# Two query tiles share one output projection in a local-attention loop, and the feed-forward's stages are placed anew

## The chip, the cores and the metric

The program runs on one core of a Trainium2 chip. A core has five engines that run side by side, each with its own queue worked off in order: TensorE (PE, matrix products, with its weight loads shown apart as PEld), VectorE (DVE), ScalarE (ACT), GpSimd (POOL) and SyncE (SP), which here issues DMA transfers. Matrix products land in PSUM, a memory of eight banks; one bank holds 512 fp32 values in each of 128 partitions. The metric is the device time of one execution in microseconds (us); lower is better.

## The reference, cut to what matters

The network adds eight residual blocks to x of shape (4, 512, 128). The change touches one of them, a six-layer local transformer (`_L2_ffn_ref`):

```python
for i in range(DEPTH):                       # 6
    x = attn_layer(shift_tokens(x), Wqkv[i], q_scale[i], k_scale[i], Wo[i]) + x
    x = ffn_layer(shift_tokens(x), ln_g[i], ln_b[i], W1[i], b1[i], W2[i], b2[i]) + x
```

```python
def attn_layer(x, Wqkv, qs, ksc, Wo):
    qkv = x @ Wqkv                           # 128 -> 3 * 1024
    ...
    q = l2norm(q) * qs                       # and k; 16 heads of 64
    ...
    out = local_attention(q, k, v)           # windows of 32, each sees itself and the one before
    out = out.transpose(0, 2, 1, 3).reshape(b, n, INNER)
    return out @ Wo                          # 1024 -> 128

def ffn_layer(x, g, bln, W1, b1, W2, b2):
    ...                                      # layer norm
    hg = xn @ W1 + b1                        # 128 -> 2 * 341
    a, gate = jnp.split(hg, 2, -1)
    return a * jax.nn.gelu(gate, approximate=False) @ W2 + b2
```

The last product of the attention, `out @ Wo`, is the one whose form changes.

## The kernel before, in words

The program has a first and a middle part, the local transformer, and a last part. The first, middle and last parts are ordered by a planner (class `Plan`), from costs written into the code; they are not changed. The local transformer (`local_transformer`) is ordered by hand: its instructions go to each engine's queue in the order in which the loop at L2040 emits them.

The data of one batch row lie in `Y[b]`, features on partitions and the 512 tokens along the row; the upper 64 features stand one column to the right, which is the shift of the tokens. A row has four tiles of 128 tokens (`T.tt` = 0 to 3); with four rows and six layers there are 96 tiles. The loop over n is a pipeline. Trip n works on three tiles: T = tile n makes its queries, keys and values (`queries_or_keys` L1779, `rotate` L1791, `normalise` L1812, `values` L1849); T1 = tile n-1 turns them to features (`turned` L1830), makes its scores and the first steps of its softmax (`scores` L1876, `softmax` L1899); T2 = tile n-2 averages, divides, is turned to features and projected (`probabilities`, `average`, `normalised`, `attended`, `project_out` L1945, `residual` L1951). With two trips to drain there are 98.

A fourth worker is the feed-forward of a finished row, F. It is spread over four trips, its phases: `divmod(n - 6, 4)` gives row and phase. Each phase has two places in the trip, a first one after the queries and a second one at its end (`ff_stage` L2018):

- phase 0: first, the row is transposed and its moments are found (`ff_moments`); after the residual, the norm is applied on DVE (`ff_norm`, L523);
- phase 1: first, the norm's result is turned (`ff_turn`); second, the gates of chunks 0 and 1 with their Gelu on ACT (`ff_gate`, L1983);
- phase 2: first, the gate of chunk 2; second, the up products of chunks 0 and 1 and their multiplication on DVE (`ff_up`, L1994 and L1997);
- phase 3: first, up of chunk 2; second, the down product and its addition to Y (`ff_down`, L2006, and `add_y`, L1723).

Chunks have 128, 128 and 85 of the 341 inner features. ACT loads another table before the first Gelu of a row and goes back after the last. The last row of the last layer has its feed-forward in the last part (`last_feed_forward`).

PSUM is held in four tags. `mm` and `tr` have two single banks each: queries and keys, and transposes and values. `sc` and `av` (`pair`, with bufs=1) have one buffer of two banks each. In `sc` lie the scores, until DVE has taken the maximum (L1903) and the subtraction (L1904) from them; every feed-forward product takes `sc` too. In `av` lie the averages and then the projection.

On PE a trip runs: queries, P transposes, queries, first feed-forward step, averages, q transposes, keys, averages, k transposes, keys, attn transposes, scores, projection, values, second feed-forward step. On DVE the rotations and divisions come first, then the maximum and the subtraction, then the residual. On ACT, after the softmax's exp (L1909) come the copies of v, a Gelu of the second step, and the next trip's squares (L1788) and P copies (L1914); a rotation on DVE waits for its square.

The projection takes 8 products of 128x128 weights with 128 columns of `aT`; in fp32 PE runs two passes for each, so the profile counts 16.

Of the kernel before, what the change touches and what calls it, by code (L numbers as in the profile page):

```python
# [20 lines left out]
F32 = mybir.dt.float32  # L21
# [13 lines left out]
DEPTH, LH, LD, WIN = 6, 16, 64, 32  # L35
# [204 lines left out]
def tile_kernel(ctx: ExitStack, tc: tile.TileContext, A: dict, out: bass.AP):  # L240
    nc = tc.nc
    V, G, SC, PE, DMA = nc.vector, nc.gpsimd, nc.scalar, nc.tensor, nc.sync
# [43 lines left out]
    def p_tr(*shape):  # L286
        return psum(shape, "tr", 2)
# [54 lines left out]
    for b in range(B):  # L342
        t = xpool.tile([128, NT, D], F32, name=f"x{b}", tag=f"x{b}")
# [26 lines left out]
    with banks(), tc.tile_pool(name="prep", bufs=1) as prep:  # L370
# [26 lines left out]
        t = p_tr(128, B, SK)  # L397
# [3 lines left out]
        t = p_tr(128, 4, D)  # L401
# [3 lines left out]
        t = p_tr(128, 8)  # L405
# [3 lines left out]
        t = p_tr(128, 2, E)  # L409
# [59 lines left out]
    def col(r):  # L469
        return cols[:, r : r + 1]  # L470
# [7 lines left out]
    for i, cap in enumerate((CAP0, CAP3, CAP3)):  # L478
        n = -(-E * cap // 128)
# [101 lines left out]
    def to_features(src):  # L581

        t = p_tr(128, NT, 128)
        for i in range(NT):
            PE.transpose(t[:, i], src[:, i], ident)  # L585
        return t
# [1114 lines left out]
    def local_transformer(Y, lf):  # L1701

        with ExitStack() as es:
# [4 lines left out]
            tp = es.enter_context(tc.tile_pool(name="lt", bufs=2))  # L1708
# [3 lines left out]
            def pair(tag):  # L1712

                t = homes["pair"].tile([128, 2, 512], F32, tag=tag, bufs=1, name=f"ps_{tag}")
                return t

            def add_y(b, t, bias=None):
                for r, o in ((slice(0, 64), 0), (slice(64, 128), 1)):
                    dst = Y[b][r, o : o + S]
                    if bias is None:  # L1720
                        V.tensor_tensor(dst, t[r], dst, ALU.add)
                    else:
                        V.scalar_tensor_tensor(dst, t[r], bias[r], dst, ALU.add, ALU.add)  # L1723
# [213 lines left out]
                )  # L1937

            def attended(T):
                flat = T.attn.rearrange("p k x d -> p k (x d)")  # L1940
                T.aT = tp.tile([128, LH // 2, 128], F32, name="aT", bufs=1)
                for g in range(2):
                    SC.copy(T.aT[:, 4 * g : 4 * g + 4], to_features(flat[:, 4 * g : 4 * g + 4]))

            def project_out(T):  # L1945
                t = pair("av")[:, 0, :128]
                for c in range(8):
                    PE.matmul(t, T.wo[:, c], T.aT[:, c], start=(c == 0), stop=(c == 7))  # L1948
                T.out = t

            def residual(T):  # L1951
                t = T.out
                for r, o in ((slice(0, 64), 0), (slice(64, 128), 1)):
                    dst = Y[T.b][r, 128 * T.tt + o : 128 * T.tt + o + 128]
                    V.tensor_tensor(dst, t[r], dst, ALU.add)


            def ff_moments(F):
                F.t = pair("sc")[:, 0].rearrange("p (a b) -> p a b", b=128)
                for tt in range(NT):  # L1960
                    PE.transpose(F.t[:, tt], Y[F.b][:, 128 * tt : 128 * tt + 128], ident)
                F.xn = lnp.tile([128, NT, D], F32, name="xn")
                SC.copy(F.xn, F.t)
                F.found = moments(F.xn)

            def ff_norm(F):
                layernorm(F.xn, F.xn, F.found)
# [11 lines left out]
            def ff_gate(F, *chunks):  # L1979
                t = pair("sc")  # L1980
                for j, c in enumerate(chunks):
                    n, o = CH_W[c], DI + 128 * c
                    PE.matmul(t[:n, j], F.w1[:, o : o + n], F.xnT, start=True, stop=True)  # L1983
                for j, c in enumerate(chunks):
                    n = CH_W[c]
                    SC.activation(
                        F.h[:n, c], t[:n, j], AF.Gelu, bias=col(R_B1 + (3 + c) * DEPTH + F.i)[:n]
                    )

            def ff_up(F, *chunks):  # L1990
                t = pair("sc")
                for j, c in enumerate(chunks):
                    n, o = CH_W[c], 128 * c
                    PE.matmul(t[:n, j], F.w1[:, o : o + n], F.xnT, start=True, stop=True)  # L1994
                for j, c in enumerate(chunks):
                    n = CH_W[c]
                    V.scalar_tensor_tensor(  # L1997
                        F.h[:n, c], t[:n, j], col(R_B1 + c * DEPTH + F.i)[:n], F.h[:n, c],
                        ALU.add, ALU.mult,
                    )  # L2000

            def ff_down(F):
                t = pair("sc")[:, 0]
                for c in range(3):
                    n = CH_W[c]
                    PE.matmul(t, F.w2[:n, c], F.h[:n, c], start=(c == 0), stop=(c == 2))  # L2006
                add_y(F.b, t, col(R_B2 + F.i))
# [10 lines left out]
            def ff_stage(F, phase, second):  # L2018
                F.w1, F.w2 = loaded[F.i][3:5]
                if phase == 0 and not second:  # L2020
                    ff_moments(F)
                elif phase == 1:
                    ff_gate(F, 0, 1) if second else ff_turn(F)
                elif phase == 2 and second:
                    ff_up(F, 0, 1)
                elif phase == 2:
                    ff_gate(F, 2)
                    SC.preload_act_table_set(EXP_LN)
                elif phase == 3:
                    ff_down(F) if second else ff_up(F, 2)  # L2030

            tiles = [Tile(i, b, tt) for i in range(DEPTH) for b in range(B) for tt in range(NT)]
# [2 lines left out]
            tabs = {0: tables(loaded[0][5])}  # L2037
            swap(0)
            SC.preload_act_table_set(EXP_LN)
            for n in range(len(tiles) + 2):  # L2040
                T = tiles[n] if n < len(tiles) else None
                T1 = tiles[n - 1] if 0 <= n - 1 < len(tiles) else None
                T2 = tiles[n - 2] if 0 <= n - 2 < len(tiles) else None
                m, phase = divmod(n - 6, 4)
                F = rows[m] if 0 <= m < len(rows) else None
                if T:
                    if n % 16 == 7 and T.i + 1 < DEPTH:
                        loaded[T.i + 1] = load(T.i + 1)
                    if n == 4:
                        fill, send, send_back = clear(lnp, 1)  # L2050
                        fill(G)
                        send(DMA)
                        send_back(DMA)
                    if n % 16 == 15 and T.i + 1 < DEPTH:
                        tabs[T.i + 1] = tables(loaded[T.i + 1][5])
                    T.before = tiles[n - 1] if T.tt else None
                    T.w, T.wv, T.wo = loaded[T.i][:3]
                    T.tabs = tabs[T.i]
                    queries_or_keys(T, 0, 0)
                if T2:  # L2060
                    probabilities(T2)
                if T:
                    queries_or_keys(T, 0, 1)
                    rotate(T, 0, 0)
                if F:
                    ff_stage(F, phase, False)
                if T2:
                    average(T2, 0)
                if T1:
                    turned(T1, 0)  # L2070
                if T:
                    queries_or_keys(T, 1, 0)
                if T2:
                    normalised(T2, 0)
                if T:
                    rotate(T, 0, 1)
                if T2:
                    average(T2, 1)
                if T1:
                    turned(T1, 1)  # L2080
                if T:
                    queries_or_keys(T, 1, 1)
                if T2:
                    normalised(T2, 1)
                if T:
                    rotate(T, 1, 0)
                if T2:
                    attended(T2)
                if T and T.tt == NT - 1 and n + 1 < len(tiles):
                    swap(tiles[n + 1].b)  # L2090
                if T1:
                    scores(T1)
                if T:
                    rotate(T, 1, 1)
                if T:
                    normalise(T)
                if T1:
                    softmax(T1)
                if T2:
                    project_out(T2)  # L2100
                    residual(T2)
                if F and phase == 0:
                    ff_norm(F)
                if T:
                    values(T, 0)
                    values(T, 1)
                if F:
                    ff_stage(F, phase, True)
# [95 lines left out]
    with ExitStack() as stay:  # L2204
        yp = stay.enter_context(tc.tile_pool(name="y", bufs=1))
        Y = []
# [32 lines left out]
```

## Time and profile before

| | us |
|---|---|
| median of three runs | 2434.31 (2431.93 to 2436.33) |
| the profiled execution | 2475.2 |
| its span, first to last instruction | 2473.4 |
| PE busy | 2242.8 (91%) |
| DVE busy | 1745.4 (71%) |
| ACT busy | 1291.9 (52%) |
| POOL busy | 1383.7 (56%) |
| L1948, projection, PE | 198.0 in 1536 passes |
| L1786, queries and keys, PE | 398.0 in 768 passes |

In a row of the profile come the line of the code, the engine, what is written and read with its shape, the count, the busy time and the mean of one in ns, and after the second bar the idle time of the engine before these instructions with what ended it. Matmuls overlap one another, so the distance between the starts of two says more than the duration of one. In a timeline the first two numbers are the start and the time until the merged instructions ended, in us; a bracket at the end is the engine's idle time before them and what released it.

### The profile page before, as it was taken

How to read it: one execution, taken by the hardware profiler on the slowest of the kernel's cores; microseconds unless marked ns; L12 is line 12 of the kernel's file. 1: busy time of each engine (PE TensorE's matmuls, PEld its weight loads, DVE VectorE, ACT ScalarE, POOL GpSimd, SP SyncE). 2: the span in 40 equal slices, each digit the busy share in tenths (PEclk: the TensorE clock that was granted, in tenths of full speed). 3: DMA queues.
4: the chain of work that ended last, by engine and by line, in shares of the span. 5: the costliest groups of instructions: out<-in, count | busy, mean ns of one | idle time of the engine just before them, and what ended most of it. 6: DMA issues, size and time to landing. Idle time of an engine off the chain costs nothing.

```text
span 2473.4 us, 86733 instructions
## 1 busy us (share of the span) xinstructions
PE 2242.8 (91%) x37341; PEld 1478.8 (60%) x37341; DVE 1745.4 (71%) x3818; ACT 1291.9 (52%) x2379; POOL 1383.7 (56%) x1948
## 2 busy tenths in 40 slices
PE   7959879968999999999999999999999999988686
PEld 3527644536666666666666666666666666644364
DVE  5626355757788888877887888888888888765522
ACT  3523225535666556666666666566666666533232
POOL 2242232446667666676667667766667666532433
PEclk9969989989999999999999999999999999989688
DMA  7210110015411121111211121111211111120022
GB/s 161 87 42 21 36 42 2 1 51 102 118 29 35 31 60 50 26 35 35 70 35 31 33 79 32 30 35 29 76 35 32 30 35 34 30 78 10 23 75 82
DMA packets 134297, 116.14 MB, mean 47 GB/s; under 512 B 29505, under 2 KB 102700, under 8 KB 133916
## 3 DMA queue, kind: packets, MB, share of 16 engines
q1 hardware_dynamic: 128373, 102.81, 16.0%
q0 software_dynamic: 4608, 7.35, 0.9%
q8 instruction: 296, 4.85, 0.8%
q14 instruction: 85, 0.70, 0.1%
q10 hardware_dynamic: 935, 0.43, 0.1%
HBM read 42.84 MB, written 21.52 MB: 26 GB/s over the span
## 4 chain that ended last, share of the span: by engine, by line
PE 71%; DVE 15%; issue 4%; DMA 3%; POOL 3%; ACT 2%; another core or an unknown queue 1%; SPq 1%; POOLq 0%; DVEq 0%; ACTq 0%
PE ps_tr L585 12%; PE ps_mm L1786 11%; PE ps_av L1948 6%; PE ps_av L1924 5%; PE ps_tr L1863 5%; PE ps_sc L1893 4%; DVE xn L523 3%; PE ps_sc L1994 2%; PE ps_sc L2006 2%; PE ps_sc L1983 2%; PE ps L776 2%; PE ps L1315 2%; PE ps L1687 2%; PE ps L785 2%; PE ps L1571 1%
## 5 line engine op out<-in xcount | busy, mean ns | idle before, releaser
L1809 POOL TENSOR_TENSOR rc<-rc,rs 128x512 f32<-128x512 f32 x384 | 489.8, 1276 | 382.7 <-DVE rs L1799 324.0
L1786 PE MATMUL ps_mm<-wqk,y 128*128 128x512 f32 x768 | 398.0, 601 | 10.4 <-DVE rs L1799 7.0
L1828 POOL TENSOR_TENSOR rc<-rc,rn_y 128x512 f32<-128x512 f32 x384 | 388.6, 1044 | 7.5
L1796 DVE TENSOR_TENSOR rc<-ps_mm,tabs 128x512 f32<-128x512 f32 x384 | 262.3, 683 | 139.1 <-ACT sq L1788 124.7
L1788 ACT ACTIVATE sq<-ps_mm 128x512 f32<-128x512 f32 x384 | 231.2, 603 | 167.0 <-PE ps_mm L1786 119.2
L1799 DVE TENSOR_TENSOR rs<-ps_mm,tabs 128x512 f32<-128x512 f32 x384 | 261.2, 680 | 0.3
L1808 DVE TENSOR_REDUCE ss<-sq 128x8 f32<-128x512 f32 x384 | 259.3, 675 | 0.0
L585 PE MATMUL ps_tr<-cst,rc 128*128 128x128 f32 x1536 | 211.7, 281 | 7.3 <-issue 4.1
L1924 PEld LDWEIGHTS ps_av<-v,PT 64*32 64x32 f32 x12288 | 138.4, 105 | 124.8 <-PE ps_tr L585 54.9
L1948 PE MATMUL ps_av<-aT,wo 128*128 128x128 f32 x1536 | 198.0, 281 | 4.3 <-issue 4.2
L1948 PEld LDWEIGHTS ps_av<-aT,wo 128*128 128x128 f32 x1536 | 179.5, 191 | 13.5 <-issue 4.6
L585 PEld LDWEIGHTS ps_tr<-cst,rc 128*128 128x128 f32 x1536 | 166.0, 142 | 27.9 <-issue 6.0
L1924 PE MATMUL ps_av<-v,PT 64*32 64x65 f32 x12288 | 170.3, 225 | 5.1 <-DVE attn L1934 1.1
L1893 PE MATMUL ps_sc<-kT,qT 64*32 64x64 f32 x12288 | 146.0, 224 | 25.3 <-issue 24.6
L1020 POOL DMA_INDIRECT back<-ye,to x80 | 78.0, 975 | 160.3 <-DVE ye L1134 117.7
L1786 PEld LDWEIGHTS ps_mm<-wqk,y 128*128 128x128 f32 x768 | 124.9, 193 | 60.5 <-issue 49.7
L1893 PEld LDWEIGHTS ps_sc<-kT,qT 64*32 64x32 f32 x12288 | 139.6, 105 | 35.1 <-issue 28.9
L766 ACT ACTIVATE P<-ps,deltaT 77x512 f32<-77x512 f32 x192 | 115.0, 684 | 69.2 <-PE ps L760 61.8
L1909 ACT ACTIVATE P<-P 128x1024 f32<-128x1024 f32 x96 | 101.5, 1057 | 90.9 <-DVE P L1904 90.9
L1820 ACT ACTIVATE rn_y<-ss 128x32 f32<-128x32 f32 x96 | 22.0, 229 | 236.6 <-POOL ss L1819 236.6
L1840 ACT COPY qT<-ps_tr 128x512 f32<-128x512 f32 x192 | 103.3, 589 | 75.4 <-PE ps_tr L585 75.1
L1840 ACT COPY kT<-ps_tr 128x512 f32<-128x512 f32 x192 | 103.4, 590 | 66.3 <-PE ps_tr L585 66.2
(410 smaller groups left out, 4414.3 us busy)
## 6 DMA issues: line engine op xcount, KB each, us to landing
v<-v SPq DMA_DIRECT2D x432, 65.0 KB
v<-v SPq DMA_DIRECT2D x96, 195.0 KB
wqk<-in_L_ffn_Wqkv_dram SPq DMA_DIRECT2D x24, 256.0 KB
sent<-xn SPq DMA_DIRECT2D x2, 2210.0 KB
xe<-sent SPq DMA_DIRECT2D x16, 260.0 KB
back<-xn SPq DMA_DIRECT2D x2, 2048.0 KB
raw<-in_L_ffn_W_dram SPq DMA_DIRECT2D x8, 512.0 KB
yb<-back SPq DMA_DIRECT2D x16, 256.0 KB
```

The source lines that it names most:

```text
L585: PE.transpose(t[:, i], src[:, i], ident)
L1786: PE.matmul(t, lhs, T.w[2 * kind + c], start=True, stop=True)
L1788: SC.activation(sq, t, AF.Square)
L1796: V.tensor_tensor(a, t, bc(T.tabs[:, 2 * kind, tt], [128, 8, LD], 1), ALU.mult)
L1799: V.tensor_tensor(r.rearrange("p h (x d) -> p h x d", x=2), t.rearrange("p h (x d) -> p h x d", x=2)[:, :, ::-1], bc(T.tabs[:, 2 * kind + ...
L1808: V.tensor_reduce(T.ss[:, kind, 8 * c : 8 * c + 8], sq, AX.X, ALU.add)
L1809: G.tensor_tensor(a, a, r, ALU.add)
L1828: G.tensor_tensor(a, a, bc(y[:, o : o + 8], [128, 8, LD], 2), ALU.mult)
L1840: SC.copy(t[:, 4 * c : 4 * c + 4, lead:], to_features(T.rot[kind, c].rearrange("p (k x) d -> p k (x d)", x=2)),)
L1893: PE.matmul(T.banks[32 * w : 32 * w + 32, z, k], T.qT[r, k, 32 * w : 32 * w + 32], T.kT[r, k, 32 * w : 32 * w + 64], start=False, stop=Tru ...
L1924: PE.matmul(T.means[32 * w : 32 * w + 32, x0, k], T.PT[r, 4 * g + k, 32 * w : 32 * w + 32], (T.v1 if w % 2 else T.v2)[r, x0, 4 * g + k], s ...
L1948: PE.matmul(t, T.wo[:, c], T.aT[:, c], start=(c == 0), stop=(c == 7))
```

## The change

Two tiles with T.tt = 0, 1 or 2, 3 now share one `aT` of 256 columns: `attended` writes the half that belongs to its tile. `project_out` and `residual` run in the trips with odd T2.tt only, over 256 columns. With n = T2's index + 2 these are the odd n. The feed-forward starts at n - 7, one trip later, and there is one more trip to drain it, 99 in all. Its up products are dealt out in another way: chunk 0 at the end of phase 2, chunks 1 and 2 in the first place of phase 3. So phase 0 and 2 fall on odd n, phase 1 and 3 on even n.

```diff
             def attended(T):
+
                 flat = T.attn.rearrange("p k x d -> p k (x d)")
-                T.aT = tp.tile([128, LH // 2, 128], F32, name="aT", bufs=1)
+                if T.tt % 2 == 0:
+                    T.aT = tp.tile([128, LH // 2, 256], F32, name="aT", bufs=1)
+                else:
+                    T.aT = T.before.aT
+                o = 128 * (T.tt % 2)
                 for g in range(2):
-                    SC.copy(T.aT[:, 4 * g : 4 * g + 4], to_features(flat[:, 4 * g : 4 * g + 4]))
+                    SC.copy(
+                        T.aT[:, 4 * g : 4 * g + 4, o : o + 128],
+                        to_features(flat[:, 4 * g : 4 * g + 4]),
+                    )
 
             def project_out(T):
-                t = pair("av")[:, 0, :128]
+
+                t = pair("av")[:, 0, :256]
                 for c in range(8):
                     PE.matmul(t, T.wo[:, c], T.aT[:, c], start=(c == 0), stop=(c == 7))
                 T.out = t
 
             def residual(T):
-                t = T.out
-                for r, o in ((slice(0, 64), 0), (slice(64, 128), 1)):
-                    dst = Y[T.b][r, 128 * T.tt + o : 128 * T.tt + o + 128]
+                t, o0 = T.out, 128 * (T.tt - 1)
+                for r, o in ((slice(0, 64), o0), (slice(64, 128), o0 + 1)):
+                    dst = Y[T.b][r, o : o + 256]
                     V.tensor_tensor(dst, t[r], dst, ALU.add)
...
                 elif phase == 2 and second:
-                    ff_up(F, 0, 1)
+                    ff_up(F, 0)
...
                 elif phase == 3:
-                    ff_down(F) if second else ff_up(F, 2)
+                    ff_down(F) if second else ff_up(F, 1, 2)
...
-            for n in range(len(tiles) + 2):
+            for n in range(len(tiles) + 3):
...
-                m, phase = divmod(n - 6, 4)
+                m, phase = divmod(n - 7, 4)
...
-                if T2:
+                if T2 and T2.tt % 2:
                     project_out(T2)
                     residual(T2)
```

## The prediction

> **What bounds the kernel now.** I read the page's chain first: it says which engine the end hangs on.
>
> ```profile
> PE 71%; DVE 15%; issue 4%; DMA 3%; POOL 3%; ACT 2%; another core or an unknown queue 1%; SPq 1%; POOLq 0%; DVEq 0%; ACTq 0%
> L1948 PE MATMUL ps_av<-aT,wo 128*128 128x128 f32 x1536 | 198.0, 281 | 4.3 <-issue 4.2
> ```
>
> TensorE (PE) carries 71% of it, and the line to be changed, L1948, is on it. Next, four trips of the local loop as windows (start:end, length, busy us of each engine, granted clock, DMA share, GB/s): n = 47, 48, 49, 50, which are the old feed-forward phases 1, 2, 3, 0.
>
> ```profile
> 1321.20:1339.50 18.30, 17.17 (x333) 11.50 (x332) 15.43 (x25) 12.50 (x23) 16.67 (x26) 1.00 0.12 32
> 1339.55:1356.25 16.70, 16.70 (x331) 11.17 (x330) 11.79 (x20) 12.37 (x22) 10.22 (x15) 1.00 0.13 35
> 1356.26:1373.80 17.54, 17.54 (x333) 11.55 (x332) 13.99 (x23) 8.95 (x17) 12.72 (x19) 1.00 0.09 25
> 1373.83:1388.60 14.77, 14.62 (x329) 10.62 (x328) 14.14 (x30) 7.69 (x16) 9.14 (x14) 1.00 0.15 40
> ```
>
> PE is full, at full clock; VectorE (DVE) has a few us free. A trip's length is its PE work plus any PE wait. Trip n=6 starts at 625.79 and n=94 at 2115.28, so 22 rounds of four trips average 67.70. Last, the timeline of trip n=48 (start, us, engine, line):
>
> ```profile
> 1349.55 1.46 PE L1893 MATMUL ps_sc<-kT,qT 64*32 64x64 f32 x128
> 1350.93 2.05 PE L1948 MATMUL ps_av<-aT,wo 128*128 128x128 f32 x16
> 1351.16 1.22 DVE L1903 TENSOR_REDUCE la_mx<-ps_sc 128x16 f32<-128x1024 f32 x1
> 1352.41 1.22 DVE L1904 TENSOR_TENSOR P<-ps_sc,la_mx 128x1024 f32<-128x1024 f32 x1
> 1352.82 1.02 PE L1863 MATMUL ps_tr<-wv,y 128*128 128x512 f32 x2
> 1353.55 0.58 DVE L1955 TENSOR_TENSOR y<-ps_av,y 64x128 f32<-64x128 f32 x2
> 1353.68 1.02 PE L1863 MATMUL ps_tr<-wv,yw 128*128 128x512 f32 x2
> 1354.54 1.88 PE L1994 MATMUL ps_sc<-xnT,lw 128*128 128x512 f32 x4
> 1356.26 1.02 PE L1786 MATMUL ps_mm<-wqk,y 128*128 128x512 f32 x2
> ```
>
> See the order on PE: scores (until 1350.93), projection (1.89 to the next start), values (1.72), then the trip's second feed-forward step. That step writes `ps_sc`, the one buffer that the scores filled; DVE empties it with the maximum and the subtraction, until 1353.55. The step could start at 1354.54 without a wait only because projection and values had filled 3.61 us.
>
> **The projection.** Two groups of 16 passes over 128 columns become one of 16 passes over 256. The passes of L1948 start 0.112 apart, those of 512-column rows such as L1786 0.429 apart: linear in the columns. So 256 columns take 0.2145, a group 3.43, against 2 x 1.89 = 3.78: -0.35 a pair, -0.70 a round. Here a rule speaks louder for the change: the Trainium skill, "TensorE: Matmul & The Clock Gate", Back-to-back issue gap, gives a sustained 81 ns a matmul at N=128 and 131 at N=512, which would put 256 columns only some 20% over 128. Scaled to this row, that estimate is 0.135 a pass, 2.17 a group, -3.2 a round (-71 us in all). The 512-column rows here cost 3.8 times the 128-column ones, not 1.6 times, so I take 0.2145 and keep 0.135 as the far end. Upwards, a slow first pass (the second now starts 0.21 after the first) would add 0.1.
>
> **The rest of the edit.** The aT copies are as many and as long. The residual adds become two of 64x256 per pair, for four of 64x128 (0.29 each in L1955). A 64x512 row of DVE takes 0.75, so about 0.42: 0.84 per pair for 1.16, on DVE, which is not the bound. No DMA is added or moved; the even trips' queues on SP and POOL are unchanged.
>
> **The new trips.** Odd n carry the projection, even n none. Phase 0 falls on n = 3 mod 4, then 1, 2, 3 on n = 0, 1, 2. The base of a trip with neither projection nor feed-forward is 16.70 - 1.89 - 0.95 (the 85-column gate or up with its gap) - 1.72 = 12.14, of which 10.43 up to the scores' end (1350.93 - 1339.55 - 0.95).
>
> - Phase 0 (n=3): the old trip with a wider projection, 14.77 + 1.54 = 16.31.
> - Phase 1 (n=0): 12.14 + turn 0.5 + gate 1.72 = 14.36 of PE work. But now only the values (1.72) stand between the scores and the gate. The tail of the profile, where a trip has no values, shows the bare hand-over:
>
> ```profile
> 2158.47 2.05 PE L1948 MATMUL ps_av<-aT,wo 128*128 128x128 f32 x16
> 2158.58 1.23 DVE L1903 TENSOR_REDUCE la_mx<-ps_sc 128x16 f32<-128x1024 f32 x1 [3.14 <-PE ps_sc L1893]
> 2159.91 1.23 DVE L1904 TENSOR_TENSOR P<-ps_sc,la_mx 128x1024 f32<-128x1024 f32 x1
> 2161.28 1.10 PE L1994 MATMUL ps_sc<-xnT,lw 128*128 128x512 f32 x2 [0.76 <-DVE P L1904]
> ```
>
> From the scores' end (2158.47) to the step on the same buffer (2161.28) it is 2.81 with DVE idle beforehand, so at least 1.09 of wait. DVE is later here: in the trip before, scores end at 11.16 (n=50), the wide projection 3.43 later, DVE sees it 0.3 after that, adds for 0.84 and norms for 3.45 (the chain's usual `xn` piece): 19.2, or 2.9 into this trip. The rotations start then and take 8.84 (n=51: 1392.28 to 1401.12) to the maximum, 11.75; the scores end at 10.93. From the maximum's start to the release is 2.61 (2.47 to the subtraction's end in n=48, and 0.14 from there to PE in the tail). Lag 0.82 + 2.61 - 1.72 is a wait of 1.71. Trip: 16.1.
> - Phase 2 (n=1): 12.14 + 3.43 + 0.95 + up 0.86 = 17.38. The gate's late start delays ACT, which queues exp, v copies, table load, gelus, then the squares and the P copies of the next trip: 4.5 from exp to the squares (n=47/48), now begun 1.7 before the trip's end, not 2.7. In n=48 the gelus were done at 1.9 and the first P copy at 2.8; with 1.0 on each, `ps_sc` is free at 2.9, 0.34 after the 85-column gate wants it (2.59), and the averages behind it find their P copy (3.8). Trip: 17.7.
> - Phase 3 (n=2): 12.14 + up of two 1.81 + down 2.58 = 16.53; two multiplications of DVE ahead of the rotations put the maximum at 12.55, the scores end at 12.24, so the wait behind the values is 0.31 + 2.61 - 1.72 = 1.20. Queued behind it on PE is the whole next trip. Trip: 17.7.
>
> Here the rule against the change stands: "Perfetto Trace Analysis", Optimizing Tensor Performance, wants independent matmul groups on different banks, so that emptying one overlaps the next. Taken alone it would expose the whole 2.81 twice a round, 5.6; the row shows the values covering 1.72 each time, so I charge 1.71 + 1.20.
>
> **What is gained back.** In phase 1 the old loop waited 0.75 a round: 0.43 for the v copies (n=51: P transposes at 1389.90, queries' 0.86 over at 1389.46; the chain softmax, exp, v copy was longer than the PE work over it) and 0.31 for the norm. With a wider projection over both, that goes. PE also halts for "issue" inside the scores, some 1.35 a round (start-to-start distances beyond their usual value, summed); in the even trips DVE's lag swallows about 0.28 of it.
>
> Old round: work 14.77 + 16.26 + 16.71 + 17.57 = 65.31, waits 0.75, issue 1.35, 0.3 unnamed: 67.70. New: 16.31 + 16.07 + 17.72 + 17.73 = 67.83, issue 1.07, 0.3: **69.2**. Per round +1.5, in 22 rounds +32 us.
>
> **The ends.** Before, n=6 to the loop's last add takes 1551.1 (625.79 to 2176.85): 22 rounds and 61.6. After: a bare trip n=6, 12.1; 22 rounds; n=95 as phase 0, 16.3; then a tail. The old tail, from trip 96's first transpose, is 28.2. The new one: averages at 3.4, scores' end 10.2, hand-over 2.8, gate until 14.7; gelus and P copy hold the last averages to 17.3; 6.3 to the old projection's end, 1.5 more for the wide one, 25.1; then up, multiply, up, multiply, down and add alone, 7.9: 33.0. Sum 61.4: nothing in total, though the extra trip costs 4.8.
>
> The sum stands against the profiled execution (2475.2, span 2473.4), which is 41 us above the median of the runs, 2434.3. The difference carries over: **+32** on the median, 2466.
>
> **Rivals.** *Cheap wide passes* (the other side): should a 256-column pass cost 0.135, the round loses 2.5 more and ends 1.1 below the old one: -24 us, 2410. It decides from 0.169 a pass down (1.47 over 32 passes). For it speaks the skill's table, against it the linear rows. 8%.
> *The waits spread*: ACT's lateness in phase 2 also delays the squares, and DVE starts its rotations at 3.4 in place of 2.4. I let the projection cover that; if not, each round loses about 1 more: 2488. For it: ACT is 12.4 busy in such a trip, in one chain. Against: DVE would have 3.4 us of projection before PE asks. 12%.
> *Waits half as large*: 1.45 less a round, which is no change, 2434. For it: a lag that dissolves in a round's slack. Against: 1.09 of each hand-over is fixed. 5%.
> The forecast itself: 75%, its own range 2448 to 2484: a quarter of the two hand-over waits and 0.1 on each wide group, either way (0.7 + 0.2 a round, 20 us), a little rounded down since both will hardly fall one way. That the edit does not do what it says I set aside: the width is in the slice.
>
> **How the numbers follow.** Some 0.2% (5 us) is what a measurement can tell from none. Slower: 75 + 12 + half of the 5 = 88%; same 4%; faster 8%. The range for 8 in 10 leaves out the fast case and part of the slowest: 2440 to 2490.
>
> **What would show it.** Wide passes start 0.21 apart. The second-step gate and down rows (L1983, L2006 by today's numbering) follow the values with a wait on the subtraction, 1.7 and 1.2 us, in every even trip; the up row in odd trips has none. Trips run about 16.3, 16.1, 17.7, 17.7. The wait on v copies is gone from phase 1. PE's busy share falls. I am wrong if those rows follow the values at once, or if passes start under 0.17 apart.

## The result, and the profile after

The changed kernel takes 2487.67 us, median of four runs (2485.24 to 2488.97), against 2433.12 (2427.50 to 2436.33) for the kernel before: a ratio of 1.0233 (1.0215 to 1.0251), slower by 54.6 us. The forecast was +32 and 2466, with a range of 2440 to 2490; the result lies 2.3 us inside its upper end.

The profiled execution of before had its first and last part some 47 us longer than that of after, so the two spans (2473.4 and 2485.1) can't be subtracted; the local loop can be compared. From the first queries to the last addition it takes 1652.3 before and 1711.1 after, **+58.8**. Of this, the 22 rounds of four trips take +53.4 (67.70 to 70.13 each), the ends +5.9, and the first six trips -0.4.

First the page of the changed kernel: the shares of the chain that ended last, and from the costliest groups the four that the change touches. Lines have moved: the projection is L1957, the residual L1964, the gate L1992, up L2003, its multiplication L2006, down L2015.

```profile
PE 67%; DVE 20%; issue 5%; POOL 3%; ACT 2%; DMA 2%; SPq 1%; POOLq 0%; ACTq 0%; DVEq 0%
L1957 PE MATMUL ps_av<-aT,wo 128*128 128x256 f32 x768 | 180.5, 387 | 5.1 <-issue 5.1
L1964 DVE TENSOR_TENSOR y<-ps_av,y 64x256 f32<-64x256 f32 x96 | 40.6, 423 | 51.9 <-PE ps_av L1957 51.2
L1992 PE MATMUL ps_sc<-xnT,lw 128*128 128x512 f32 x138 | 72.0, 631 | 23.5 <-DVE P L1904 23.5
L2015 PE MATMUL ps_sc<-fh,lw 128*128 128x512 f32 x138 | 64.8, 605 | 26.4 <-DVE P L1904 24.9 <-DVE fh L2006 1.6
```

PE's share of the chain fell from 71 to 67%, and DVE's rose from 15 to 20%: the end now hangs on DVE in places where it hung on PE. The last two rows tell where. Before the gate and the down product PE stands idle for 23.5 and 24.9 us, until `P` of L1904, the subtraction that empties the scores' buffer, is done. In the kernel before, the same two rows waited for nothing of the kind:

```profile
L1983 PE MATMUL ps_sc<-xnT,lw 128*128 128x512 f32 x138 | 66.9, 594 | 1.0 <-ACT fh L1986 1.0
L2006 PE MATMUL ps_sc<-fh,lw 128*128 128x512 f32 x138 | 63.0, 592 | 0.0
```

The projection did get cheaper: 180.5 us busy in 768 passes for 198.0 in 1536.

Next, four trips of the loop as windows (start:end, length, busy us of each engine, granted clock, DMA share, GB/s): n = 80 to 83, the new phases 1, 2, 3, 0.

```profile
1892.40:1908.70 16.30, 14.96 (x317) 9.54 (x316) 14.24 (x21) 10.19 (x19) 10.86 (x16) 1.00 0.14 36
1908.71:1926.54 17.83, 17.83 (x329) 12.07 (x328) 12.06 (x20) 13.30 (x23) 13.17 (x19) 1.00 0.09 24
1926.55:1944.68 18.13, 16.98 (x319) 10.15 (x318) 13.37 (x21) 8.95 (x17) 10.41 (x15) 1.00 0.12 33
1944.69:1961.13 16.44, 16.32 (x329) 11.91 (x328) 15.32 (x32) 9.57 (x18) 11.37 (x18) 1.00 0.13 34
```

In the two even trips, the first and the third row, PE is busy for 14.96 of 16.30 and 16.98 of 18.13: the missing 1.3 and 1.15 us are one wait each. The odd trips are as full as before. The timeline of n=80 has the wait of the first row (it begins within the scores, of which it shows 112 of 128 passes):

```profile
1902.32 1.35 PE L1893 MATMUL ps_sc<-kT,qT 64*32 64x64 f32 x112
1903.59 1.12 PE L1863 MATMUL ps_tr<-wv,y 128*128 128x512 f32 x2
1904.30 1.22 DVE L1903 TENSOR_REDUCE la_mx<-ps_sc 128x16 f32<-128x1024 f32 x1
1904.56 1.02 PE L1863 MATMUL ps_tr<-wv,yw 128*128 128x512 f32 x2
1905.55 1.22 DVE L1904 TENSOR_TENSOR P<-ps_sc,la_mx 128x1024 f32<-128x1024 f32 x1
1906.92 1.96 PE L1992 MATMUL ps_sc<-xnT,lw 128*128 128x512 f32 x4 [1.34 <-DVE P L1904]
1908.71 1.02 PE L1786 MATMUL ps_mm<-wqk,y 128*128 128x512 f32 x2
```

The scores are over at 1903.59, where the values start. DVE comes to the maximum only at 1904.30, 0.71 late, and needs 2.62 from there until the gate may write (1906.92). The values fill 1.99 of it, from 1903.59 to their last pass at about 1905.58. In the kernel before, the projection lay in this gap too.

### The profile page after: what moved, and what is told of

Read it like the earlier page. It is cut to its first block, busy times and chain, and to the rows that moved or that the text cites. A ratio compares the mean times of both kernels' runs of the same rounds, so it can differ in the third digit from the quotient of the medians.

```text
span 2485.1 us, 85079 instructions
## 1 busy us (share of the span) xinstructions
PE 2230.0 (90%) x36573; PEld 1447.2 (58%) x36573; DVE 1729.9 (70%) x3722; ACT 1300.3 (52%) x2379; POOL 1380.3 (56%) x1948
## 4 chain that ended last, share of the span: by engine, by line
PE 67%; DVE 20%; issue 5%; POOL 3%; ACT 2%; DMA 2%; SPq 1%; POOLq 0%; ACTq 0%; DVEq 0%
PE ps_tr L585 11%; PE ps_mm L1786 10%; PE ps_av L1957 7%; PE ps_av L1924 5%; PE ps_sc L1893 4%; PE ps_sc L1992 3%; PE ps_tr L1863 3%; DVE rc L1796 3%; PE ps_sc L2015 3%; DVE rs L1799 3%; DVE ss L1808 2%; DVE P L1904 2%; PE ps_sc L2003 2%; DVE la_mx L1903 2%; PE ps L1315 2%
## 5 line engine op out<-in xcount | busy, mean ns | idle before, releaser
L585 PE MATMUL ps_tr<-cst,rc 128*128 128x128 f32 x1536 | 211.2, 280 | 4.5 <-POOL rc L1828 3.0
L1924 PEld LDWEIGHTS ps_av<-v,PT 64*32 64x32 f32 x12288 | 138.8, 105 | 127.4 <-PE ps_tr L585 54.1
L1957 PE MATMUL ps_av<-aT,wo 128*128 128x256 f32 x768 | 180.5, 387 | 5.1 <-issue 5.1
L585 PEld LDWEIGHTS ps_tr<-cst,rc 128*128 128x128 f32 x1536 | 165.7, 142 | 24.9 <-POOL rc L1828 4.6
L1924 PE MATMUL ps_av<-v,PT 64*32 64x65 f32 x12288 | 170.6, 225 | 6.8 <-issue 2.4
L1957 PEld LDWEIGHTS ps_av<-aT,wo 128*128 128x128 f32 x768 | 142.2, 190 | 27.7 <-issue 6.2
L1934 DVE TENSOR_TENSOR attn<-ps_av,la_den 128x512 f32<-128x512 f32 x192 | 132.8, 691 | 6.6
```

Of the source, the lines that this page charges most:

```text
L1924: PE.matmul(T.means[32 * w : 32 * w + 32, x0, k], T.PT[r, 4 * g + k, 32 * w : 32 * w + 32], (T.v1 if w % 2 else T.v2)[r, x0, 4 * g + k], s ...
L1934: V.tensor_tensor(T.attn[:, 4 * g : 4 * g + 4].rearrange("p k x d -> p x k d"), T.means[:, :, :, 0:LD], bc(den, [128, 2, 4, LD], 3), ALU.mult,
```

## The experiments

The loop's length and its rounds come from one profile of each kernel, and ratios from runs side by side with the kernel before. The kernel before took 2437.1 beside the runs e1, e2, e3 and e5, 2436.24 beside e6 to e9, and 2483.72 beside e10, where both kernels were longer. The longer part lies outside the local loop: the profile of e10 has 826.7 us there and that of the kernel before, which is as long, 821.1, for 773 to 780 in the other nine; the cause is not known. One profile is one execution, so a loop's length can be off by some us from that of the median.

### Which half of the edit costs: pairing alone, placing alone

Pairing alone is the changed kernel with the feed-forward where it was:

```diff
-            for n in range(len(tiles) + 3):
+            for n in range(len(tiles) + 2):
-                m, phase = divmod(n - 7, 4)
+                m, phase = divmod(n - 6, 4)
-                    ff_up(F, 0)
+                    ff_up(F, 0, 1)
-                    ff_down(F) if second else ff_up(F, 1, 2)
+                    ff_down(F) if second else ff_up(F, 2)
```

> The paired projection alone; the feed-forward stays at n - 6 with its old dealing of the up products, so phase 0 and 2 fall on the even trips, which have no projection. Theory (what a trip's end needs is cover behind the scores: 2.8 us for the score buffer, and nearly 5 us, counted from the scores' end, until P can be transposed, because exp and the two v copies must come first): gate and down sit behind the wide projection and wait for nothing, the up pair of phase 2 waits some 1.2, and after the phase-0 trip, which ends with the values alone, the P transposes wait some 2.3. Against that 0.4 less projection and 0.4 less of the old waits: round about 69.8 to 70.3, time 2475 to 2490. Rival A (the shift of the stages is what costs, pairing is a small gain): 2420 to 2430. Rival B (the pairing costs by itself, whatever the stages do): near 2488, with waits in places other than the two named.

Placing alone is the kernel before with the same four lines the other way round, so that every trip keeps its own projection.

> The stages begin one trip later and up is dealt out as 0 and then 1 and 2, but every trip keeps its own projection of 128 columns. Theory: every second step still has 3.6 us of projection and values in front of it, so none waits for the score buffer; the rounds stay at 67.7 and only the drain of one more trip is added, about 5 us: 2436 to 2446. Rival A (the shift costs): 2465 to 2490. Rival B: near 2433.

Pairing alone took 2490.32, ratio 1.0211 (1.0193 to 1.0230), at the upper edge of what was expected. Placing alone took 2454.23, ratio 1.0076 (1.0059 to 1.0093). So **the pairing carries the loss**. The new places are no worse for a paired projection than the old ones: with the old ones, other things wait, as the waits of PE in the pairing alone show (engine, buffer and line, what it waited for: us, times, longest).

```profile
PE ps_tr L585 <- ACT v L1864: 46.9, 25, 2.1
PE ps_sc L2003 <- DVE P L1904: 20.3, 23, 2.7
```

L585 is the P transposes at the head of a trip. Without a projection between scores and values, the chain from the scores over subtraction, exp and v copies sticks out by 2 us each round. A second cost comes with it: after nine of these waits, each of 2.07 us, the clock was granted at 0.50 for 3.41 us (the window of one, with the clock as the third figure from the right). From these figures it is an estimate of at most 15 us in all.

```profile
1324.39:1327.80 3.41, 3.41 (x12) 2.27 (x12) 1.88 (x3) 1.94 (x5) 3.41 (x6) 0.50 0.00 0
```

Placing alone was expected at 2436 to 2446 and missed. In its profile the rounds take 68.15, +0.45, or 9.9 in all, the ends +4 and the first six trips +0.8. No feed-forward step waits in it more than twice. What grew is PE's idle time for "issue", here of the kernel before and then of placing alone:

```profile
PE ps_sc L1893 <- issue: 24.6, 26, 1.5
PE ps_av L1948 <- issue: 4.2, 7, 1.2
PE ps_av L1924 <- issue: 0.8, 1, 0.8
```

```profile
PE ps_sc L1893 <- issue: 35.6, 28, 3.3
PE ps_av L1948 <- issue: 2.7, 5, 0.7
PE ps_av L1924 <- issue: 1.0, 2, 0.7
```

The three rows make 29.6 and 39.3 in the whole program. Counted within the 22 rounds and from start to start, as the last experiment below does, they grew by 10.0, as much as the rounds. These are halts of mostly about 1 us inside long rows of small passes; here three of them, in n = 23, 39 and 55, took 2.4 to 3.3. What slowed the other executions is not in this trace: it is of the quickest of six (2443.47, at a mean granted clock of 0.963; the others took up to 2457.93, at 0.957 to 0.961).

### Is it the cover? The kernel before with less of it

The theory says that the wait has nothing to do with the pair's width or the feed-forward's phase, only with how much PE work stands between the scores and the next writer of their buffer. So I left both as they were before and moved the second step ahead of the values:

```diff
+                if F:
+                    ff_stage(F, phase, True)
                 if T:
                     values(T, 0)
                     values(T, 1)
-                if F:
-                    ff_stage(F, phase, True)
```

> The kernel before, without pairing or shift; only the second feed-forward step of each trip is put ahead of the values, so that the projection's 1.89 us alone lies between the scores and the step. Theory: hand-over of 2.61 plus a lag of 0.2 to 0.8 against 1.89 of cover, so waits of 0.9 to 1.5 in phases 1, 2 and 3, some 3 a round: 2490 to 2510. Rival (the cover is not what counts): 2430 to 2440.

It took 2500.46, ratio 1.0268 (1.0245 to 1.0291), and the wait on the subtraction stands in all three second steps (gate L1983, up L1994, down L2006), which had none to speak of before:

```profile
PE ps_sc L1983 <- DVE P L1904: 23.3, 23, 1.5
PE ps_sc L1994 <- DVE P L1904: 14.5, 21, 0.9
PE ps_sc L2006 <- DVE P L1904: 14.1, 20, 0.7
```

With the projection alone as cover (1.89 between starts) the three waits average 1.01, 0.69 and 0.71. The changed kernel's two, with the values alone as cover (1.72), are 1.02 and 1.13 in the same view. So too little cover makes this wait by itself, without pairing and without the shift.

### The other remedy: another buffer

If the one two-bank buffer is what the step waits for, the step shouldn't wait in another. In the even trips `av` is free between the averages and the next trip's, since no projection is in it. The changed kernel with the gate of two chunks and the down product in `av`:

```diff
             def ff_gate(F, *chunks):
-                t = pair("sc")
+                t = pair("av" if len(chunks) == 2 else "sc")
...
             def ff_down(F):
-                t = pair("sc")[:, 0]
+                t = pair("av")[:, 0]
```

> The changed kernel, but the gate of two chunks and the down product write the averages' buffer in place of the scores' one; in even trips nothing else uses it by then. Theory: both waits on the subtraction (1.0 to 1.5 and 0.9 to 1.4) vanish from the second step. Part of it comes back one step later: after gate, PE runs on to the P transposes 1.1 us earlier, and exp, v copies, table load and gelus on ACT are no earlier than before, so P transposes wait some 0.6 and the averages of the phase-2 trip about 1.2 more. Net 0.7 to 1.2 a round: 2460 to 2475. Rival A (the buffer is not what the step waits for): no change, 2485 to 2490. Rival B (the wait is worth its full 2.5 a round): 2433.

It took 2458.92, ratio 1.0089 (1.0064 to 1.0114): about 29 us less than the changed kernel, as its loop says (1681.9 for 1711.1); 5 of these are fewer halts (36.7 for 41.8, counted as in the last experiment). Both waits on the subtraction are gone; undisturbed trips of phases 1 and 3 take 14.50 and 16.64 for 15.57 and 18.15. But phase 2 went from 17.83 to 18.82: in it the averages (L1924) now wait for the copy of P, 26.3 us in all. The timeline of n=57 shows why:

```profile
1477.43 1.05 ACT L1864 COPY v<-ps_tr 128x512 f32<-128x512 f32 x2
1478.50 1.28 ACT L1995 ACT_TABLE_LOAD   x1
1479.79 1.26 ACT L1995 ACTIVATE fh<-ps_av,cols 128x512 f32<-128x512 f32 x2
1480.95 0.60 ACT L1788 ACTIVATE sq<-ps_mm 128x512 f32<-128x512 f32 x1
1481.43 1.08 ACT L1914 COPY PT<-ps_tr 128x512 f32<-128x512 f32 x2
1482.07 1.01 PE L1924 MATMUL ps_av<-v,PT 64*32 64x65 f32 x64 [1.16 <-ACT PT L1914]
```

ACT runs v copies, table load, Gelus, a square and P copies without a gap, and PE, which now comes to the averages earlier, waits for the end of that chain. Next I took work off ACT: first the v copies of even trips to DVE, then also the P copies of the phase-2 trips.

```diff
-                SC.copy(T.v1[:, x0, :, 0:LD], t)
+                copy(V if T.tt % 2 == 0 else SC, T.v1[:, x0, :, 0:LD], t)
```

> As e3_av_bank, and in the even trips DVE copies v in place of ACT. Theory (what came back in e3_av_bank, 0.3 for the P transposes and 1.16 for the averages' P copy, came from ACT's chain exp, v copies, table load, gelus): ACT's chain is shorter by 1.05, so the averages wait about 0.1 to 0.3 in phase 2, rounds fall by 0.7 to 1.2, time 2433 to 2448. Rival (what is left over comes from elsewhere): 2455 to 2462.

```diff
-                    probabilities(T2)
+                    probabilities(T2, V if F and phase == 2 else SC)
```

> As e8_v_on_dve, and in phase-2 trips DVE makes the P copies too, since ACT has two gelus in front of them there and DVE stands idle until the first square. Theory: the last wait that pairing brought, 0.3 to 0.8 of the averages for the P copy in phase 2, goes; that trip falls from 18.5 to about 17.9 and the round from 67.7 to 67.1: 2420 to 2430, 0.3 to 0.6% under the kernel before. Rival (the remaining time is PE's own work and its halts for issue): 2434 to 2440.

The first took 2437.45, ratio 0.9999 (0.9984 to 1.0015): the whole loss is made good, and the averages' wait fell from 26.3 to this:

```profile
PE ps_av L1924 <- ACT PT L1914: 8.0, 19, 1.1
```

The second took 2479.33 where the kernel before took 2483.72, ratio 0.9977 (0.9963 to 0.9992). Its expectation in microseconds, 2420 to 2430, was written for the level of the earlier runs and missed; in relation to the kernel before it had promised 0.3 to 0.6% and gave 0.2%, while its round, 67.20, came out as expected (67.1). Neither of ACT's waits is left among its costly ones, and phase 2 is back at 17.52, its bare PE work. The loops of the two profiles, 1645.0 for 1652.3, point the same way. So the paired projection is worth something, some 0.2%, but only with its second steps in another buffer and with six copies a round fewer on ACT; it is the one version here that beats the kernel before.

### Cover for every trip: half a wide projection in each

Here the projection of a pair is cut after four of its eight weight blocks: half is done in the pair's own odd trip, half in the next even trip, each half with its own residual additions; `aT` gets a second buffer, and the up products are dealt as before. Every trip again has some 1.7 of projection behind its scores.

```diff
-            def project_out(T):
+            def project_out(T, half):
-                for c in range(8):
-                    PE.matmul(t, T.wo[:, c], T.aT[:, c], start=(c == 0), stop=(c == 7))
+                for c in range(4 * half, 4 * half + 4):
+                    PE.matmul(t, T.wo[:, c], T.aT[:, c], start=(c % 4 == 0), stop=(c % 4 == 3))
...
-                if T2 and T2.tt % 2:
-                    project_out(T2)
-                    residual(T2)
+                T3 = tiles[n - 3] if 0 <= n - 3 < len(tiles) else None
+                for P_, half in ((T2, 0), (T3, 1)):
+                    if P_ and P_.tt % 2:
+                        project_out(P_, half)
+                        residual(P_)
```

> Pairing kept, but its 16 wide passes are cut in two halves of four chunks: 8 passes at the end of the odd trip and 8 at the end of the next even trip, each with its own residual add of 256 columns; up is dealt out as before the change. So every trip again has some 1.8 us of projection behind its scores and 3.5 with the values. Theory (missing cover in the even trips is what costs): the waits for the score buffer and those on ACT go, rounds of 67.2 to 68.2, and with the longer drain 2430 to 2450. Rival (pairing itself costs: wide passes, the shared aT, the later residual): 2470 to 2490.

It took 2453.78, ratio 1.0081 (1.0058 to 1.0104), a little above what was expected. The waits behind the scores are gone, as they should be. What is new is the turn (L1981), which waits for the norm on DVE:

```profile
PE ps_sc L1981 <- DVE xn L523: 16.5, 36, 0.7
```

The norm ends 19.47 into its trip, for 18.42 in the kernel before (medians of 22). The addition ahead of it is wider, 0.85 for 0.58, and the first of the norm's four pieces takes 1.16 for 0.35; why that piece is slower is not shown. So giving the cover back takes away most of the loss, and these 16.5 us of what is left hang on an engine that was not the bound.

### The dealing of the up products

Phase 3 came out 0.4 us longer than forecast. This timeline of the changed kernel, n=50, shows its up products of two chunks and the multiplications on DVE:

```profile
1372.27 1.88 PE L2003 MATMUL ps_sc<-xnT,lw 128*128 128x512 f32 x4
1374.19 1.41 DVE L2006 SCALAR_TENSOR_TENSOR fh<-ps_sc,cols,fh 128x512 f32<-128x512 f32 x2 [0.94 <-PE ps_sc L2003]
```

Both multiplications start after both products, 4.51 into the trip, and DVE comes to the maximum at 12.88, where the forecast had 12.55. That makes the wait of the down product longer. With the old dealing (two up products at the end of phase 2, one in phase 3) the head of phase 3 should lose that:

```diff
-                    ff_up(F, 0)
+                    ff_up(F, 0, 1)
...
-                    ff_down(F) if second else ff_up(F, 1, 2)
+                    ff_down(F) if second else ff_up(F, 2)
```

> The changed kernel with the old dealing of the up products (0 and 1 at the end of phase 2, 2 in the first place of phase 3). Theory: in phase 3 the two multiplications wait for both products of one buffer and push DVE's whole chain back, so that the maximum starts 0.78 behind the scores; with one product DVE is 0.6 to 0.8 earlier and PE 0.86 earlier, the lag stays or falls to 0.3, and the wait for the down product falls from 1.43 to about 1.0: 0.2 to 0.5 a round, 2477 to 2484. Rival (the dealing is what costs): 2440 to 2460. Rival (dealing is of no weight): 2486 to 2489.

It took 2486.77, ratio 1.0196 (1.0179 to 1.0214), for the 2477 to 2484 expected. In microseconds that is the time of the changed kernel (2487.67), by the ratios it is 0.4% less, by the loops 2.6 us (1708.5 for 1711.1). The mechanism is there, the gain hardly: down's wait fell from 24.9 to 17.8 us,

```profile
PE ps_sc L2015 <- DVE P L1904: 17.8, 22, 1.0
```

and phase 3 by 1.33 where undisturbed (18.15 to 16.82), of which 0.86 went to phase 2 with the up product itself. Of the 0.47 that should be left, the rounds show 0.20 (69.93 for 70.13). Halts took 0.15 of the rest (45.2 for 41.8 in the 22 rounds, by the count of the next experiment); 0.1 stays unexplained.

### The halts: 128 instructions more ahead of the loop

The kernel before, with 32 tiny fp32 products ahead of the loop whose result nothing reads. This is extra work of a few us at most; every PE instruction of the loop moves by 128 places (weight loads and passes counted).

```diff
             SC.preload_act_table_set(EXP_LN)
+            shim = p_tr(128, 8, LD)
+            for _ in range(32):
+                PE.matmul(shim[:32, 0, :8], ident[:, :32], ident[:, :8], start=True, stop=True)
             for n in range(len(tiles) + 2):
```

> The kernel before with 32 tiny products, 128 PE instructions, ahead of the loop; nothing reads them. Question: the halts for issue inside the scores, 26 of about 1 us before and 30 in the changed kernel, and more in e2_shift_alone, which was 10 us slower than its waits explain. If they come at fixed counts of PE instructions (the distances between them are 1280, 2048 and sums of these), the halts move to other trips and the time moves by up to 10 us either way beyond the 3 us of the products. If they belong to certain places of the code, the same trips halt and the time is 2436 to 2441.

It took 2443.54, ratio 1.0042 (1.0025 to 1.0058). The halts are in other trips than before, and there are more of them:

```profile
PE ps_sc L1893 <- issue: 29.9, 29, 2.3
PE ps_av L1948 <- issue: 7.7, 10, 2.4
PE ps_av L1924 <- issue: 4.7, 4, 2.3
```

What the halts are stands in the DMA records of the traces. The page of the changed kernel counts a queue that carries instructions (packets, MB, share of the 16 DMA engines):

```profile
q8 instruction: 290, 4.75, 0.8%
```

Its packets have 16 KB, and there is one for every 256 PE instructions: 231 for 59,091 in the 22 rounds of the kernel before. A packet starts 1.0 us after PE has entered a block of 256 and has landed 2.1 us after it (medians). Of 411 halts over 0.15 us in the loops of the eleven traces, 407 stand at the same place of such a block, in e9 too, where the loop has moved by 128. At each of these PE goes on 1.1 to 1.7 us after a packet has landed; at the ends of blocks without a halt it had landed some 4 us before (medians). So PE stands there because its next instructions have not come. The scores are 128 passes and as many weight loads in 1.46 us, so a block that falls into them is used up before the next one is there.

Their cost can be taken at the ends of the blocks, as what the distance between two starts exceeds its median over the 22 rounds. It is 31.8 us in the 22 rounds of the kernel before, 41.8 in the changed kernel, 41.8 in placing alone and 42.5 here; so 10.7 of the 14.0 by which the rounds grew here. A shift by 128 moves the ends of the blocks within the trip: onto work that waits, where a late packet costs nothing, or onto a dense row, where it does.

## Why the prediction was right, and why it fell short

**Right: the sign and its cause.** A wait on the subtraction in each even trip, behind the values, because the projection no longer stands there. It was forecast at 1.71 and 1.20. Counted in the same way, against a cover of 1.72, it is 1.21 (1.02 to 1.92) in phase 1 and 1.39 (1.02 to 1.53) in phase 3, together 0.3 less than forecast. e7 shows it without pairing, e3 and e6 show it gone with another buffer or another cover. The rule in the Trainium skill, "Perfetto Trace Analysis", Optimizing Tensor Performance (independent groups on different banks), which I weighed against the change, was the right one: following it gave back 29 of 55 us in e3.

**Right: the wide pass.** It starts every 0.216 (forecast 0.2145; the two sustained figures of the Trainium skill, "TensorE: Matmul & The Clock Gate", Back-to-back issue gap, which the rival calls its table, would by estimate have made it 0.135). The whole group takes 3.56, not 3.43, since one start in it comes 0.1 late, as the prediction had priced from above. The cheap-pass rival fell with this row. The residual is 0.423 twice, as forecast.

**Right: what was gained back in phase 1.** Of the old waits, those on v copies fell from 4.1 to 1.5 us in the 22 rounds and those on the norm from 2.3 to none. And phase 2, undisturbed, is 17.83 = 17.51 of work and 0.32 of wait (forecast 17.7 with 0.34).

**Nearly right: work and waits of the round.** The undisturbed trips of the four phases sum to 67.99, the forecast's work and waits to 67.83, in part by luck: phase 1 is 0.5 shorter (DVE comes 0.11 to 0.71 behind the scores, forecast 0.82) and phase 3 0.4 longer. The step of phase 3 that failed is "two multiplications of DVE ahead of the rotations put the maximum at 12.55": they start together and late, and the maximum is at 12.88.

**Wrong: the halts.** The sentence "in the even trips DVE's lag swallows about 0.28 of it" was to bring the halts from 1.35 to 1.07 a round. Inside the scores they went up, from 1.38 to 1.67, summed as the prediction did. In all rows, at the ends of the blocks, they rose by 0.45 a round (31.8 to 41.8 in the 22 rounds). The waits of PE in the changed kernel, for the three rows of the kernel before above:

```profile
PE ps_sc L1893 <- issue: 29.5, 29, 3.1
PE ps_av L1957 <- issue: 5.1, 5, 1.6
PE ps_av L1924 <- issue: 2.4, 3, 1.0
```

The mean round stands 2.14 above the undisturbed trips, where halts and the unnamed rest had been put at 1.37: 0.77 too little. The halts rose by 0.45 where they were to fall by 0.28, which is 0.73 of it. With the 0.16 from work and waits this is the round's +0.93, or 20 us in 22 rounds: most of the miss. e2 and e9 show that an edit that only moves the instructions can do this; which way it goes for a given edit I could not have read from the profile of before.

**Wrong: the ends.** They were to sum to nothing and cost 5.9: 0.3 in n=6, 1.6 in n=95 (a halt of 0.9 in it), and 4.1 in the tail, 37.15 for 33.0. The tail's timeline shows two terms:

```profile
2180.95 1.67 PE L1893 MATMUL ps_sc<-kT,qT 64*32 64x64 f32 x128
2185.36 3.75 PE L1992 MATMUL ps_sc<-xnT,lw 128*128 128x512 f32 x4 [2.74 <-DVE P L1904]
2188.91 1.91 PE L585 MATMUL ps_tr<-cst,P 128*128 128x128 f32 x8
2202.27 1.98 PE L2003 MATMUL ps_sc<-xnT,lw 128*128 128x512 f32 x4 [1.53 <-DVE fh L2006]
2205.82 2.84 PE L2015 MATMUL ps_sc<-fh,lw 128*128 128x512 f32 x6 [1.57 <-DVE fh L2006]
```

The bare hand-over left PE idle for 2.74 (forecast 2.8 from the scores' end), but the gate behind it runs at half pace, 3.75 for the usual 1.96, and so do the transposes. And from the wide projection's end to the last addition it takes 10.5, not 7.9, with two waits on the multiplications.

**The rival that gave 2488.** Its number is nearly the result, its mechanism isn't: undisturbed, phase 2 has no wait beyond the 0.32. The halts and the ends came to the same size by chance. The result lies outside the forecast's own range (2448 to 2484) and within the wider one, in which this rival had its place.

Three figures of the forecast are off without weight: the subtraction ended at 1353.63, not 1353.55; 75, 12 and half of 5 make 89.5%, not 88; and cheap wide passes would have ended 1.0 below the old round, about -23 us, not 1.1 and -24.

## What to carry to other kernels

An operation that only fills time on the busiest engine may be the cover of a hand-over behind it: before moving it, look for the next writer of the buffer that is being emptied meanwhile, and price the hand-over from the scores' end to that writer. If the operation must move, give the writer another buffer, then follow the chain that becomes late next; here it took two such steps, to ACT and to DVE, until the saving showed. And where PE halts for its instructions, as in this loop, an edit that moves them can gain or lose by that alone: here it lost 10 us three times, in the changed kernel, placing alone and e9, which a forecast should carry as uncertainty.

## What the runs showed of the hardware

- **Halts for instructions.** PE's instructions come by DMA, 256 in a packet of 16 KB. In dense rows of 64-column passes PE uses up a block before the next has landed and halts, mostly for about 1 us. At the ends of blocks this cost 31.8 to 42.5 us in the 22 rounds of before, after, e2 and e9, and 128 instructions ahead of the loop moved the time by 0.42%.
- **The clock after a wait.** Windows of the changed kernel's tail give the granted clock (the third figure from the right):

```profile
2173.07:2185.36 12.29, 9.02 (x301) 6.93 (x301) 6.38 (x10) 5.77 (x11) 1.80 (x4) 0.96 0.18 46
2185.36:2189.20 3.84, 3.84 (x6) 1.67 (x7) 0.00 (x0) 2.27 (x3) 0.00 (x0) 0.50 0.00 0
2189.20:2191.00 1.80, 1.80 (x9) 1.64 (x8) 0.00 (x0) 1.80 (x4) 0.00 (x0) 0.50 0.00 0
```

  With one wait of 2.74 us the clock fell to half, and it stayed so for over 5 us of work after it. The waits of up to 1.66 us within the rounds of this kernel left it at 1.00. In pairing alone, waits of 2.07 us did not always: after nine of fifteen in the rounds the clock stood at 0.50 for 3.41 us.
- **The first passes after a switch.** One start in a group of wide passes comes 0.10 late, and the second values pass does so too where the values follow the scores at once: some 0.4 a round in small change that no row of the page names.
